# An attention kernel over embedding rows: another layout of the tiles, no loop, and one gather in 256 replaced by row fetches

## The chip, the core and the metric

The kernel runs on one core of one Trainium2 chip. A core has engines that run their own instruction streams in order and meet through semaphores: TensorE (PE, matrix products), VectorE (DVE, elementwise work, 32x32 transposes, statistics), ScalarE (ACT, activations and copies), GpSimd (POOL, here the engine that issues indirect DMAs) and SyncE (SP, here the engine that issues plain DMAs). SBUF is the on-chip memory of 128 partitions, PSUM the accumulator memory that TensorE writes. The metric is the device time of one execution in microseconds (us); before the change the median of three runs is 32846.29 us.

## What is computed

A user's history of 200 items is weighted by a small network ("attention unit") against a candidate item, and the weighted sum goes through a three-layer head. The batch is 16384, the history length L is 200, an embedding row has D = 64 floats, and the item table has 100000 rows. `dice` is an activation with a mean and a variance over the batch.

```python
def dice(x, alpha, axis):
    mean = jnp.mean(x, axis=axis, keepdims=True)
    var = jnp.var(x, axis=axis, keepdims=True)
    p = jax.nn.sigmoid((x - mean) * jax.lax.rsqrt(var + EPS))
    return x * (p + alpha * (1.0 - p))
u, it, c = u_emb[user], i_emb[item], c_emb[cate]
h = i_emb[hist]                                     # (200, 16384, 64)
itb = jnp.broadcast_to(it[None], h.shape)
feat = jnp.concatenate([h, itb, h - itb, h * itb], axis=-1)
a = dice(feat @ au_W1 + au_b1, au_alpha, axis=1)    # 36 hidden units, moments over the batch
w = a @ au_W2 + au_b2
cur = jnp.sum(w * h, axis=0)
z = jnp.concatenate([u, it, c, cur], axis=-1)
z = dice(z @ W1 + b1, alpha1, axis=0)
z = dice(z @ W2 + b2, alpha2, axis=0)
return z @ W3 + b3
```

## The kernel before

**Tiling.** The batch is cut into ND = 8 chunks of 2048 rows; a chunk is a tile of 128 partitions by TD = 16 rows. One *step* k handles one chunk c of one history position l (k = 8 l + c), so there are 1600 steps. `ts(c, TD)` names the columns of a chunk.

**Prologue.** `table_rows` and `table_store` go through the item table in 49 blocks and write a DRAM tensor `table` whose row is the embedding (64 floats) and its product with the part of the first attention layer that depends on the history item alone (64 floats: 36 units and padding). At the same time POOL gathers the candidate item, user and category rows (3 x 8 x 16 gathers, `fetch_one`), and `keep_one` transposes them and stores them to DRAM (`xi`, `ucT`) or keeps them (`itT`). All transposes of this part (`transpose`, `transpose_back`, L223 and L231) work on 64 partitions, four instructions for a tile.

**A step.** `fetch(k)` issues 16 indirect DMAs on POOL (`gather`, L202), each of which brings 128 rows of `table` (512 B each) into `land[k % 12]`, and one plain DMA on SP (L369) that brings the item's part of the layer, `xi[c]`, into `xit[k % 2]`. Once the rows have landed, `turn` (L377, four transposes of 64 partitions by 1024 elements) brings them into the layout with features on partitions, `product` multiplies by the item and runs the matrix product into PSUM tile `px`, on top of `xit`, which ACT has copied there (L458). `hidden` adds the two parts of the hidden layer and takes batch statistics (L390, L392). When the eight chunks of a position are done, `moments` makes scale and shift from the statistics. Eight to ten steps later `weigh(k-10)` (L398 to L415 on DVE, after two activations on ACT, L448 and L451) applies dice, sums over the hidden units, and adds weight times row to `cur`. The gather of step k writes the buffer that tile k-12 has used; the last reader of that is `weigh(k-12)`, which runs in step k-2.

**Order.** All instructions are in a hand-written order (`manual_schedule`). The first 168 history positions run in a hardware loop, `For_i` at L498, of 24 positions an iteration (7 iterations); the last 32 are written out. `fetch_ids` (L213, SP) loads the indices of the next position once in eight steps; it waits until the gathers of the position before have read the index buffer.

**Head.** During the written-out steps the parts of the first head layer that don't depend on `cur` are computed (`base_of_layer1`, scratch tile `zt`). After the last gather the pipeline drains in ten steps that also do layer 1 (`layer1`, `keep1`), then layer 2 runs chunk by chunk (dice on ACT and DVE, four pairs of matrix products, L595 and L525 to keep the result and its statistics), then layer 3 (L604) and the store.

Of the kernel before, what the change touches and what calls it, by code (L numbers as in the profile page):

```python
# [20 lines left out]
LPB = 24  # L21
LAND = 12
EARLY = 4
# [5 lines left out]
def din_kernel(  # L29
# [50 lines left out]

    parts = [(0, S), (S, A - S)]

# [3 lines left out]
    blk_h = once.tile([P, P], F32, name="blk_h")  # L86
    blk_i = once.tile([P, P], F32, name="blk_i")
    blk_m = const.tile([P, P], F32, name="blk_m")
    au_w = once.tile([P, 4, A], F32, name="au_w")
    au_bias = const.tile([P, 1], F32, name="au_bias")  # L90
    au_al = const.tile([P, 1], F32, name="au_al")
    au_1al = const.tile([P, 1], F32, name="au_1al")
    au_w2 = const.tile([P, 1], F32, name="au_w2")
# [4 lines left out]
    for e in range(2):  # L98
        rows = au_W1.rearrange("(g d) a -> d g a", d=D)[e * S : (e + 1) * S]
        for g in range(2):  # L100
            r = quarter(e, g)
            nc.sync.dma_start(au_w[r], rows)
            for q, (a0, n) in enumerate(parts):
                c, a = quarter(q, g, n), slice(a0, a0 + n)
                nc.vector.tensor_add(blk_h[r, c], au_w[r, 0, a], au_w[r, 2, a])
                nc.vector.tensor_sub(blk_i[r, c], au_w[r, 1, a], au_w[r, 2, a])
                nc.vector.tensor_copy(blk_m[r, c], au_w[r, 3, a])
    for g in range(2):
        for q, (a0, n) in enumerate(parts):
            r, a = quarter(q, g, n), slice(a0, a0 + n)  # L110
            nc.sync.dma_start(au_bias[r], col(au_b1)[a])
            nc.sync.dma_start(au_al[r], col(au_alpha)[a])
            nc.sync.dma_start(au_w2[r], au_W2[a])
# [11 lines left out]
    idx = [const.tile([P, NT], I32, name=f"idx{i}") for i in range(IDX)]  # L125
    stats = [const.tile([P, 2 * ND, nc.vector.BN_STATS_DIM], F32, name=f"st{i}") for i in range(2)]
    rstds = [const.tile([P, 1], F32, name=f"rs{i}") for i in range(2)]
    shifts = [const.tile([P, 1], F32, name=f"sh{i}") for i in range(2)]
    px, pz = (psum.tile([P, CD], F32, name=n) for n in ("px", "pz"))
# [6 lines left out]
    ucT = dram.tile([2, ND, P, CD], F32, name="ucT")  # L136
# [72 lines left out]
    def load_ids(t, ids):  # L209
        nc.sync.dma_start(t, ids.rearrange("(p n) -> p n", n=NT))  # L210

# [3 lines left out]
    def by_tile(t, i):  # L215

        return t[:, ts(i, CH)].rearrange("p (n t) -> p n t", t=S)

    def transpose(dst, rows, n=TD):

        for i in range(2):
            for e in range(2):
                nc.vector.transpose(  # L223
                    by_tile(dst[ts(e, D)], i)[:, :n], rows[ts(i, D), :n, ts(e, S)]
                )

    def transpose_back(rows, src, n=TD):

        for i in range(2):
            for e in range(2):  # L230
                nc.vector.transpose(  # L231
                    rows[ts(i, D), :n, ts(e, S)], by_tile(src[ts(e, D)], i)[:, :n]
                )

    def layer(dst, pairs, n=CH, onto=False):

        for i in range(2):
            cols = slice(i * CH, i * CH + n)
# [19 lines left out]
    ids = [once.tile([P, NT], I32, name=f"ids{i}") for i in range(3)]  # L258
    for t, v in zip(ids, (r_item, r_user, r_cate)):
        load_ids(t, v)  # L260
# [11 lines left out]
    def table_rows(b):  # L272
# [11 lines left out]
        transpose(rT, tab, m)  # L284
        layer((px, pz)[b % 2], [(blk_h, rT)], n=m * S)
        tabs[b] = tab, m

    def table_store(b):
        n0, n = blocks[b]
        tab, m = tabs.pop(b)  # L290
        transpose_back(tab[:, :, D:], (px, pz)[b % 2], m)
# [9 lines left out]
    def keep_one(j):  # L301
        c, k = j % ND, j // ND
        if k == 0:
            transpose(itT[:, c], land[j % EARLY])
            layer(ph, [(blk_i, itT[:, c])])
            t = pre.tile([P, CD], F32, tag="t", name="t")
            nc.scalar.activation(t, ph, AF.Identity, bias=au_bias)
            nc.scalar.dma_start(xi[c], t)
        else:
            t = pre.tile([P, CD], F32, tag="t", name="t")  # L310
            transpose(t, land[j % EARLY])
            nc.scalar.dma_start(ucT[k - 1, c], t)
# [22 lines left out]
    with ExitStack() as main:  # L335
# [15 lines left out]
        layer(px, [(blk_m, hx[0][:, 0])])  # L351
        nc.vector.bn_stats(stats[-1 % 2][:, 0, :], hx[0][:, 0, :CH])
        for c in range(1, 2 * ND):
            nc.vector.tensor_copy(stats[-1 % 2][:, c, :], stats[-1 % 2][:, 0, :])
        for i in range(2):
            nc.vector.memset(rstds[i], 0.0)
            nc.vector.memset(shifts[i], 0.0)
        nc.sync.dma_start(xit[-1 % XI], xi[ND - 1])

# [3 lines left out]
        def x_of(k):  # L363
            return land[k % LAND][:, :, D:]

        def fetch(k):
            l, c = divmod(k, ND)
            gather(land[k % LAND], idx[l % IDX][:, ts(c, TD)], table)
            nc.sync.dma_start(xit[k % XI], xi[c])  # L369

        def turn(k):

            rows = land[k % LAND].rearrange("p n (s e c) -> p n s e c", s=2, e=2)
# [64 lines left out]
        def step(k, last=None):  # L438
# [5 lines left out]
            if has(k):  # L444
                fetch(k)
# [207 lines left out]
```

## Time and profile before

| | |
|---|---|
| runs | 32784.65, 32846.29, 32846.42 us |
| profiled execution | 32783.09 us, its span 32780.9 us |
| first gather of the program, first and last gather of `table` (start) | 9.8, 490.4, 32514.0 us |
| POOL | busy 24515.6 us, 75% of the span |
| DVE | busy 25567.4 us, 78% |
| ACT | busy 7755.2 us, 24% |
| PE | busy 6366.6 us, 19% |
| DMA | 81 GB/s over the span |

A page of the profile lists instructions by line, engine, operation, tile and shape, with the number of them, their busy time, the mean duration of one, and the idle time of the engine just ahead of them with what ended it. "issue" as the end of an idle stretch means that nothing the profile shows was waited for. A timeline lists start, duration, engine, line, operation and tiles in order of time, with the idle time in brackets. `SPq` is the queue of DMAs that SP issues.

### The profile page before, as it was taken

What the parts mean: (1) busy time and instruction counts of PE and PEld (TensorE: products, weight loads), DVE (VectorE), ACT (ScalarE), POOL (GpSimd) and SP (SyncE); (2) the same over time, 40 slices, a digit from 0 to 9 for tenths busy, and PEclk for the clock granted to TensorE, in tenths of its full rate; (3) what the DMA queues carried; (4) which work ended last, traced back from release to release, by engine and by line L of the source; (5) the groups of instructions that cost most, each with busy time, mean ns of one, the idle gap of its engine ahead of it and who ended that gap; (6) DMA issues with size and microseconds to landing.
All of it is one profiled execution on the core that took longest, in us unless ns stands there. A gap on an engine that the chain in (4) does not pass through costs nothing. (4 is left out here: it accounts for less than half of the span.)

```text
span 32780.9 us, 100656 instructions
## 1 busy us (share of the span) xinstructions
PE 6366.6 (19%) x7006; PEld 2038.0 (6%) x7006; DVE 25567.4 (78%) x28797; ACT 7755.2 (24%) x7105; POOL 24515.6 (75%) x25991
## 2 busy tenths in 40 slices
PE   3111111111111111111111111111111112221112
PEld 0000000000000000000000000000000000000000
DVE  7777777777777777777777777777777777777777
ACT  1222222222222222222222222222222222222222
POOL 7777777777777777777777777777777777777775
PEclk5555555555555555555555555555555555555555
DMA  5222222222222222222222222222222223332222
GB/s 157 80 79 79 79 79 79 79 79 79 79 80 80 79 78 79 79 79 80 79 79 79 79 79 78 79 79 80 78 79 79 79 79 85 88 90 81 79 79 60
DMA packets 1214773, 2667.86 MB, mean 81 GB/s; under 512 B 551244, under 2 KB 577388, under 8 KB 1207916
## 3 DMA queue, kind: packets, MB, share of 16 engines
q0 software_dynamic: 831488, 1691.97, 19.6%
q1 hardware_dynamic: 372012, 906.09, 9.1%
q10 hardware_dynamic: 10560, 63.79, 0.5%
q14 instruction: 692, 5.67, 0.1%
q8 instruction: 21, 0.34, 0.0%
HBM read 2590.90 MB, written 69.16 MB: 81 GB/s over the span
## 5 line engine op out<-in xcount | busy, mean ns | idle before, releaser
L202 POOL DMA_INDIRECT land<-table,idx x25600 | 24152.2, 943 | 7872.6 <-issue 7703.8
L377 DVE STREAM_TRANSPOSE hx<-land 64x1024 f32<-64x1024 f32 x6404 | 7938.2, 1240 | 6360.3 <-DMA land<-table,idx 6218.5
L240 PE MATMUL px<-hx,blk_m 128*128 128x512 f32 x6408 | 5927.6, 1080 | 26007.0 <-DVE hx L384 25941.1
L448 ACT ACTIVATE pg<-land,sh,rs 128x1024 f32<-128x1024 f32 x1610 | 1943.8, 1207 | 12980.0 <-DVE cur L415 11593.3
L454 ACT COPY ph<-hx 128x1024 f32<-128x1024 f32 x1601 | 1627.6, 1017 | 10365.2 <-DVE hx L377 10362.2
L240 PEld LDWEIGHTS px<-hx,blk_m 128*128 128x128 f32 x6408 | 1880.1, 324 | 30022.8 <-issue 29846.4
L392 DVE BATCH_NORM_STATS2 st<-land 128x6 f32<-128x512 f32 x3204 | 2060.9, 685 | 55.0
L400 DVE STREAM_TRANSPOSE hx<-pg 128x1024 f32<-128x1024 f32 x1610 | 2011.7, 1250 | 55.2
L414 DVE TENSOR_TENSOR pg<-land,ph 128x1024 f32<-128x1024 f32 x1610 | 1977.8, 1228 | 55.0
L415 DVE TENSOR_TENSOR cur<-pg,cur 128x1024 f32<-128x1024 f32 x1610 | 1970.5, 1224 | 55.6
L402 DVE TENSOR_REDUCE r<-hx 128x32 f32<-128x1024 f32 x1610 | 1964.0, 1220 | 55.3
L390 DVE TENSOR_TENSOR land<-px,hx 128x1024 f32<-128x1024 f32 x1602 | 1961.6, 1224 | 49.5
L398 DVE TENSOR_TENSOR pg<-pg,land 128x1024 f32<-128x1024 f32 x1610 | 1968.8, 1223 | 2.7 <-ACT pg L451 2.5
L384 DVE TENSOR_TENSOR hx<-ph,itT 128x1024 f32<-128x1024 f32 x1601 | 1932.0, 1207 | 0.0
L451 ACT ACTIVATE pg<-pg,au_al,au_1al 128x1024 f32<-128x1024 f32 x1610 | 1895.0, 1177 | 54.3
L458 ACT COPY px<-xit 128x1024 f32<-128x1024 f32 x1601 | 1627.2, 1016 | 383.3 <-DVE land L390 381.1
L409 DVE SCALAR_TENSOR_TENSOR ph<-r,au_bias,r 64x16 f32<-64x16 f32 x3220 | 771.3, 240 | 114.8
L406 DVE COPY r<-r 64x32 f32<-64x32 f32 x1610 | 337.2, 209 | 55.0
L448 ACT ACT_TABLE_LOAD x209 | 268.1, 1283 | 452.6 <-DVE w1a L177 314.6
L249 ACT ACT_TABLE_LOAD x203 | 260.4, 1283 | 6.7 <-PE ph L555 3.2
L249 ACT ACTIVATE std<-var,eps 128x1 f32<-128x1 f32 x201 | 59.2, 295 | 475.2 <-DVE var L435 475.2
L425 DVE COPY other<-mv 32x2 f32<-32x2 f32 x804 | 155.6, 194 | 15.1
(122 smaller groups left out, 1885.8 us busy)
## 6 DMA issues: line engine op xcount, KB each, us to landing
xit<-xi SPq DMA_DIRECT2D x1601, 512.0 KB
land<-table,idx POOLq DMA_INDIRECT x25600
table<-tab ACTq DMA_DIRECT2D x48, 1024.0 KB
tab<-in_L_rec_i_emb SPq DMA_DIRECT2D x48, 512.0 KB
zt<-ucT SPq DMA_DIRECT2D x32, 512.0 KB
idx<-in_r_hist SPq DMA_DIRECT2D x200, 64.0 KB
ucT<-t ACTq DMA_DIRECT2D x16, 512.0 KB
zbase<-zt SPq DMA_DIRECT2D x10, 512.0 KB
```

The costliest lines, as they stand in the source:

```text
L202: nc.gpsimd.indirect_dma_start(out=dst[:, n, :], out_offset=None, in_=rows, in_offset=bass.IndirectOffsetOnAxis(ap=ids[:, n : n + 1], axis=0),
L240: nc.tensor.matmul(dst[:, cols], lhsT, rhs[:, cols], start=(j == 0 and not onto), stop=(j == len(pairs) - 1), skip_group_check=onto,)
L377: nc.vector.transpose(dst.rearrange("p s (n t) -> p n s t", t=S), rows[ts(i, D), :, :, e])
L384: nc.vector.tensor_mul(hm, ph, itT[:, k % ND])
L390: nc.vector.tensor_add(x_of(k), by_row(px), by_row(hx[k % 2][:, 1]))
L392: nc.vector.bn_stats(stats[l % 2][:, 2 * c + i, :], x_of(k)[:, ts(i, TD // 2)])
L398: nc.vector.tensor_mul(by_row(pg), by_row(pg), x_of(k))
L400: nc.vector.transpose(yT, pg)
L402: nc.vector.tensor_reduce(r, yT.rearrange("p (i n u) -> p i n u", i=2, u=S), mybir.AxisListType.X, ALU.add)
L414: nc.vector.tensor_mul(by_row(pg), rows, w.unsqueeze(2).to_broadcast([P, TD, D]))
L415: nc.vector.tensor_add(cur[:, ts(c, TD)], by_row(pg), cur[:, ts(c, TD)])
L448: nc.scalar.activation(by_row(pg), x_of(k - 10), AF.Sigmoid, bias=shifts[i], scale=rstds[i])
```

## The change

Four things change together.

1. **Layout.** A row's 64 features are split in two halves `e`, and the hidden units in two parts `q`; both lie along the free axis in place of the partitions ("four groups": the four groups of 32 partitions hold four groups of batch rows). So a transpose takes all 128 partitions in one instruction in place of two or four on 64 (`halves`, `of_rows`), the matrix product of a tile is four products accumulated over `e` (`first_layer`), weights, biases and statistics get a second column for `q`, and ACT's two activations of a step become four of half the width (`gates`). The sum over hidden units needs no copy across partitions any more. `moments` gathers the four groups with small copies. `turn` writes its first transpose to PSUM (`ph`), so that ACT's copy of it goes. Two PSUM tiles `pxs` alternate by step, except in the last 144 steps.
2. **No loop.** All 1600 steps are written out.
3. **Row fetches.** In every 16th step (k % 16 == 11, up to step 1440) the 16th gather is left out. Its 128 rows are fetched by SP with 128 DMAs of one row of 512 B, eight in each of the 16 steps before: a register load of eight addresses and eight DMAs with these registers, into one of two side buffers. These, and the addresses, lie in `zt`, which is free until the head. The addresses are loaded as indices six steps ahead (`load_addresses`, SP) and multiplied by 512 (`to_addresses`, DVE). ACT copies the side buffer to the place of the missing gather.
4. **Prologue and head.** The index loads are SP's first DMAs. Layer 2 of the head keeps a chunk's result two chunks later (`keep2`), and `dice` gives half of its tensor_scalar work to ACT.

The order within a step changes: `turn` and `product`, then `gates`, then SP's row fetches and the DMA of `xit`, then `weigh`, then `hidden`, and last ACT's copy of `xit` to PSUM.

```diff
+SIDES = ((16, 11),)
+ROW = 4 * 2 * D
+    def load_addresses(q, m):
+        l, c = divmod(m * SIDES[q][0] + SIDES[q][1], ND)
+        n = c * TD + TD - 1
+        ids = r_hist[ds(l, 1), :].rearrange("l (p n) -> l n p", n=NT)[:, n : n + 1]
+            nc.sync.dma_start(addr[q][m % 2].unsqueeze(1), ids)
+    def to_addresses(q, m):
+        nc.vector.tensor_scalar_mul(addr[q][m % 2], addr[q][m % 2], ROW)
+    def side_of(k):
+        for q, (every, at) in enumerate(SIDES):
+            if k % every == at and k < L * ND - SPAN - max(SIDES)[0]:
+                return q, k // every
+        return None
...
+        def rows_by_address(q, m, part):
+            dst = side[q][m % 2].bitcast(U8)
+            n = P // SIDES[q][0]
+            engine, kind = queues[q]
+            _, at = nc.values_load_multi_w_load_instructions(
+                addr[q][m % 2][:, ts(part, n)],
+                engines=(kind,), min_val=0, max_val=ROW * (V - 1),
...
+            for j, a in enumerate(at):
+                p = part * n + j
+                engine.dma_start(dst[p : p + 1], flat[ds(a, ROW)].rearrange("(o d) -> o d", o=1))
...
         def fetch(k):
             l, c = divmod(k, ND)
-            gather(land[k % LAND], idx[l % IDX][:, ts(c, TD)], table)
-            nc.sync.dma_start(xit[k % XI], xi[c])
+            n = TD - (side_of(k) is not None)
+            gather(land[k % LAND][:, :n], idx[l % IDX][:, c * TD : c * TD + n], table)
         def turn(k):
-            rows = land[k % LAND].rearrange("p n (s e c) -> p n s e c", s=2, e=2)
-            for i in range(2):
-                for e in range(2):
-                    dst = hx[k % 2][ts(e, D), :, ts(i, CH)]
-                    nc.vector.transpose(
-                        dst.rearrange("p s (n t) -> p n s t", t=S), rows[ts(i, D), :, :, e]
-                    )
-        def product(k):
-            hm = hx[k % 2][:, 0]
+            rows = land[k % LAND]
+            hm, hw = hx[k % 2][:, 0], hx[k % 2][:, 1]
+            nc.vector.transpose(halves(ph), of_rows(rows[:, :, :D]))
             nc.vector.tensor_mul(hm, ph, itT[:, k % ND])
-            layer(px, [(blk_m, hm)], onto=True)
+            nc.vector.transpose(halves(hw), of_rows(rows[:, :, D:]))
...
         def weigh(k):
-            nc.vector.tensor_mul(by_row(pg), by_row(pg), x_of(k))
-            yT = hx[k % 2][:, 0]
-            nc.vector.transpose(yT, pg)
+            nc.vector.tensor_mul(halves(pg), halves(pg), x_of(k))
+            nc.vector.transpose(x_of(k), halves(pg))
+            r = ph[:, :TD]
             nc.vector.tensor_reduce(
-                r, yT.rearrange("p (i n u) -> p i n u", i=2, u=S), mybir.AxisListType.X, ALU.add
+                r, land[k % LAND][:, :, D:], mybir.AxisListType.X, ALU.add
             )
-            r1 = small.tile([D, 2, TD], F32, tag="r1", name="r1")
-            nc.vector.tensor_copy(r1, r[D:])
-            w = ph[:, :TD]
-            for i in range(2):
-                nc.vector.scalar_tensor_tensor(
-                    w[ts(i, D)], r[:D, i], au_bias2[:D], r1[:, i], ALU.add, ALU.add
-                )
...
-            nc.vector.tensor_mul(by_row(pg), rows, w.unsqueeze(2).to_broadcast([P, TD, D]))
+            nc.vector.scalar_tensor_tensor(
+                by_row(pg), r.unsqueeze(2).to_broadcast([P, TD, D]), au_bias2, rows,
+                ALU.add, ALU.mult,
+            )
             nc.vector.tensor_add(cur[:, ts(c, TD)], by_row(pg), cur[:, ts(c, TD)])
...
             if has(k):
                 fetch(k)
             if has(k - 1):
                 turn(k - 1)
+                if not single(k - 1):
+                    product(k - 1)
+            if has(k - 10):
+                if k % ND == 2:
+                    moments((k - 10) // ND)
+                gates(k - 10)
+            if has(k):
+                if side_of(k):
+                    q, m = side_of(k)
+                    nc.scalar.copy(land[k % LAND][:, TD - 1], side[q][m % 2])
+                for q, (every, at) in enumerate(SIDES):
+                    m, part = divmod(k + every - at, every)
+                    if side_of(m * every + at):
+                        rows_by_address(q, m, part)
+                nc.sync.dma_start(xit[k % XI], xi[k % ND])
             if has(k - 10):
                 weigh(k - 10)
+            if has(k - 2):
+                hidden(k - 2, px_of(k - 2))
+            if has(k - 1) and single(k - 1):
+                preload(k - 1)
+                product(k - 1)
+            if has(k) and not single(k):
+                preload(k)
...
-        rest_l = L % LPB + LPB
-        with tc.For_i(0, L - rest_l, LPB) as l0:
-            with tc.manual_schedule():
-                for k in range(LPB * ND):
-                    fetch_ids(k, l0, LPB + 1)
-                    step(k)
...
-        K = rest_l * ND
+        K = L * ND
...
+            for c in range(ND + 2):
+                if c < ND:
+                    activated(c)
+                if c >= 2:
+                    keep2(c - 2)
```

## The prediction

> **What bounds the kernel now.** I read three views: the groups of instructions, the timeline of one step in the middle, and the list of waits.
>
> ```profile
> L202 POOL DMA_INDIRECT land<-table,idx x25600 | 24152.2, 943 | 7872.6 <-issue 7703.8
> L377 DVE STREAM_TRANSPOSE hx<-land 64x1024 f32<-64x1024 f32 x6404 | 7938.2, 1240 | 6360.3 <-DMA land<-table,idx 6218.5
> ```
>
> The first line is the gather. Busy and idle time together are 32024.7 us, nearly the span, and what ends its idle time is "issue", so no other engine holds it. 32024.7 / 25600 = 1.251 us a gather. DVE is busy for a larger share (78%), but its idle time ends with the landing of a gather: it waits for POOL.
>
> ```profile
> 20001.18 0.94 POOL L202 DMA_INDIRECT land<-table,idx  x1 [0.30 <-issue]
> 20001.31 5.00 DVE L377 STREAM_TRANSPOSE hx<-land 64x1024 f32<-64x1024 f32 x4 [4.21 <-DMA land<-table,idx]
> 20002.43 0.94 POOL L202 DMA_INDIRECT land<-table,idx  x1 [0.30 <-issue]
> 20003.67 0.94 POOL L202 DMA_INDIRECT land<-table,idx  x1 [0.30 <-issue]
> ...
> 20015.75 1.22 DVE L415 TENSOR_TENSOR cur<-pg,cur 128x1024 f32<-128x1024 f32 x1
> ```
>
> POOL goes on every 1.25 us without a break; 16 gathers make a step of 20.0 us (DVE's next step starts at 20021.30). DVE's step ends at 20016.97, so DVE has 4.3 us to spare in each. The starts of the gathers, read through the whole timeline, keep a mean distance of 1.2482 us, and of 1.2486 in the prologue, where DVE does other work.
>
> Only a few places break this rhythm: the loop's ends, here the second of seven, and the third tile (k = 2).
>
> ```profile
> 8174.25 0.94 POOL L202 DMA_INDIRECT land<-table,idx  x1 [0.30 <-issue]
> 8184.81 1.28 ACT L448 ACT_TABLE_LOAD   x1 [20.51 <-PEq L498]
> 8184.86 5.00 DVE L377 STREAM_TRANSPOSE hx<-land 64x1024 f32<-64x1024 f32 x4 [12.21 <-PEq L498]
> 8185.88 0.94 POOL L202 DMA_INDIRECT land<-table,idx  x1 [10.69 <-issue]
> ...
> 529.13 0.94 POOL L202 DMA_INDIRECT land<-table,idx  x1 [0.30 <-issue]
> 539.53 0.94 POOL L202 DMA_INDIRECT land<-table,idx  x1 [9.45 <-issue]
> ```
>
> 8174.25 to 8185.88 is 11.63 us in place of 1.25: 10.38 lost. Five loop ends are like this, the first lost 7.1 (8.36 between starts) and the last 3.1 (4.30): 62.1 us together. At k = 2 9.15 us are lost.
>
> So the span is: first gather at 9.8, 25984 gathers at 1.248, pauses, and 266.8 us after the start of the last gather (32514.03 to 32780.9).
>
> [...] the 25600 gathers take 938, 944 and 961 ns (minimum, median, maximum) whatever DVE runs. The change's large DVE instructions read one operand from PSUM, or have one input, or are adds with `pg` in PSUM, as before. [...] the trace has 1223 (L398), so I price DVE instructions of that size by the trace's rows. [...]
>
> **The change, part by part.**
>
> *Gathers removed.* k = 11, 27, ... 1435 are 90 steps, each with one gather less: 90 x 1.2482 = 112.3 us off the bound. The instructions in program order show 25510 gathers of `table`, and the first gather of a step waits for the scalar_tensor_tensor of `weigh(k-12)` as intended, two steps back.
>
> *Loop removed.* 62.1 us off the bound. The cost could come back as stalls of POOL's instruction fetch; against it stands that the 32 positions written out in the kernel before keep 1.2482 us as well. I take all 62.1; bound 0 to 62.1.
>
> *Layout.* DVE's step before, from the timeline: 5.00 + 1.23 + 1.29 + 1.21 + 1.22 + 1.25 + 1.22 + 0.18 + 0.52 + 1.23 + 1.22 = 15.6 us. After: `turn` 1.25 + 1.21 + 1.25, `weigh` 1.22 + 1.25 + 1.22 + 1.23 + 1.22, `hidden` 1.22 + 1.29: 12.4 us. The 3.2 us saved, 5.1 ms in all, buy nothing while POOL needs 20 us a step: DVE only waits longer. If gathers became cheap, 12.4 us would be next. ACT's copy to `ph` (1.02) goes; the four half activations cost about 0.75 each (between 295 ns at one element and 1207 at 1024, L249 and L448), 3.0 in place of 2.4. `moments` now stands ahead of `gates` in one step of eight, and DVE waits there for a table load, the square root, another table load and the gates, about 8 us: 20.4 us in that step, over 20.0 by less than the 7.6 that the other steps spare, and POOL asks for that buffer only two steps later. Nothing on the path.
>
> *Row fetches on SP.* Per step one load of eight registers, eight DMAs and `xit`. A DMA costs SP 0.32 to 0.43 us (L369, L102); [...] Each DMA waits for the DMA eight before it on SP, so `xit` waits for the first row's landing, some 2 us. Both ends: 4 us if the load is cheap, 11 us at 1 us a DMA and 3 us a load. SP has the time:
>
> ```profile
> SPq L369 <- ACT px L458: 24555.0, 1391, 22.0
> SPq L213 <- DMA land<-table,idx: 6095.4, 764, 28.6
> ```
>
> It spends 15 us of a step waiting for ACT, and once in eight steps up to 28.6 us for the index buffer. Behind that wait stand the next eight rows and `xit`, which ACT needs only at the end of the step, 12 us after the same landing. ACT's copy of the side buffer could wait for late rows and hold `turn`; the last rows are asked for a step before. Cost nothing. 11520 rows of 512 B are 5.9 MB beside 2668; the 16 engines are busy 29% of the time.
>
> *Prologue.* The indices go out first on SP: the first gather comes 1.96 us after that issue as before (7.87 to 9.83), so at 0.75 + 2.0 = 2.8: 7.0 us earlier. POOL bounds the prologue too (384 gathers x 1.2486 = 479.5), so faster transposes there are hidden, and the start of the main part moves by these 7.0.
>
> *The pause at k = 2.* That gather waits for `weigh(-10)` of step 0, which stands behind DVE's memsets. There are 16 bn_stats instead of one and 15 copies: 16 x 0.645 = 10.3 in place of 1.9, so +8.4. Step 0 up to the release: before 524.40 to 539.5 = 15.1, now 3.7 + 5.1 = 8.8, so -6.3. Pause 9.15 + 2.1 = 11.3.
>
> *Tail, draining.* From DVE's start at 32518.27 to the end of layer 1's statistics at 32643.6 it takes 125.3. After: step K 12.4; step K+1 ends at 23.9 because ACT's copy and gates come after `hidden`; `moments`, roots and gates to 31.0; `weigh` and transposes 9.1 to 40.1; seven steps of 6.2 + 2.86 + 1.27 = 10.35 make 72.5; the last layer-1 part 6.2. Sum 118.8: -6.5.
>
> *Tail, layer 2.* Before, every chunk waits in a ring: PE, then ACT's keep, then ACT's sigmoid, DVE, PE again.
>
> ```profile
> 32661.12 1.11 ACT L595 ACTIVATE land<-px,z2b 80x1024 f32<-80x1024 f32 x1 [8.98 <-PE px L240]
> 32662.13 1.23 ACT L563 ACTIVATE land<-land,zshift,zrstd 128x1024 f32<-128x1024 f32 x1
> ...
> 32665.57 1.99 PE L240 MATMUL pz<-land,w2a 128*80 128x512 f32 x2 [4.49 <-DVE land L565]
> ```
>
> One chunk takes 10.4 us from matmul to matmul, of which PE needs 5.9. With the keep two chunks later PE is the limit: 8 x 5.9 = 47.4 from 32655.15, plus 2.5 for the last keep and statistics, is 32705.1 in place of 32738.8: -33.7. Layer 3 stays bound by PE (27.5 us).
>
> *Sum*, against the profiled execution: 32783.1 - 112.3 - 62.1 - 7.0 + 2.1 - 6.5 - 33.7 = 32563.6 us, -0.67%. The runs: one lies at 32784.7, with the profiled one, and two are 61.7 higher, without a reason that the profile could show. That is close to the 62.1 of the loop's ends, and it may go with them, or remain. I stay with the low basis and let the range hold both.
>
> **The rivals.**
>
> *SP becomes the bound (slower).* Place: SP's queue between two `xit`. The path has 32563.6; 1440 steps have row fetches and average 19.89 us. SP takes over above 19.89 us a step, and from 20.05 the change is slower (220 us lost over 1440 steps). [...] For it: SP runs in order, `xit` stands behind eight DMAs of a kind that no trace shows. Against: three quarters of SP's time is free.
>
> *A slower gather.* Small descriptors on the 16 engines, or DVE's other access patterns, lengthen each gather. 8.5 ns (0.7%) eat the gain; at 10 ns, 32564 + 259 = 32820, no change. Against: the spread of 938 to 961 ns, and the same distance in the prologue at 69% DMA share as at 29% in the main part.
>
> *Half the gain.* The loop's 62.1 returns as fetch stalls or the 61.7 of the slower runs stays: 32626. For it: two of three runs.
>
> **How the numbers follow.** Forecast 0.77, half the gain 0.14, slower gather 0.04, SP as bound 0.05. Forecast's own range: gather distance +-0.5 ns is +-13, tail +-15, start +-10: 32530 to 32600. With the half case 32530 to 32650, which leaves less than 2 in 10 out. No change is within 0.2% (66 us) of 32846, about what a measurement of this kernel can tell: faster 0.92, same 0.03 (most of the slower gather), slower 0.05.
>
> **What would show it.** 25510 table gathers still 1.248 us apart and "issue" ahead of them; no pause every 24 positions; DVE idle 7 us a step for a landing; SP's wait for ACT still above 8 us a step; the last gather 226.6 us ahead of the end. Wrong, if POOL's gathers wait for DVE or ACT in the middle of the span, if SP has no idle time, or if the gather's duration moves by more than 5 ns.

## The result, and the profile after

| | before | after |
|---|---|---|
| runs | 32784.65, 32845.6, 32846.29, 32846.42 us | 32621.53 to 32623.08 us (4) |
| median | 32845.94 us | 32622.44 us |
| ratio | | 0.9934, interval 0.992 to 0.9949 |
| profiled execution, its span | 32783.09, 32780.9 us | 32622.16, 32620.4 us |
| gathers of `table` | 25600 | 25510 |
| mean distance of two gathers, pauses left out | 1.2482 us | 1.2506 us |
| start of the first gather of `table`; start of the last to the end | 490.4; 266.8 us | 489.6; 210.7 us |
| DVE, POOL, ACT, PE busy | 78, 75, 24, 19% | 63, 75, 22, 30% |

The change made the kernel 0.7% faster; the forecast was 32564 us, with a range of 32530 to 32650. In the first two of the three sessions of experiments below the kernel before took some 12% longer (36.8 and 36.9 ms; the chip of the second ran it in 32.8 ms in the third), and the others with it, so a time from these is set only against the kernel before in its own session.

The groups of instructions of the kernel after (busy time, mean ns, then the idle time ahead of them and what ended it):

```profile
L215 POOL DMA_INDIRECT land<-table,idx x25510 | 24125.4, 946 | 7795.9 <-issue 7575.2
L432 DVE STREAM_TRANSPOSE ph<-land 128x1024 f32<-128x1024 f32 x1601 | 2013.6, 1258 | 10395.8 <-DMA land<-table,idx 10199.7
```

The gathers still fill POOL: 24125.4 + 7795.9 = 31921 us, all the time from the first of them to the last, and "issue" ends most of the idle time. DVE now waits 10199.7 us for landings, 6.4 us for each of the 1601 `turn`s. What is new is the last digit of the mean: 946 ns in place of 943. It looks like nothing, but the mean distance has grown by 2.4 ns (the table above), and 25900 gathers make some 62 us of that.

SyncE, which now issues eight row fetches a step, in the list of waits (total us, number, longest) and in the list of one tile's instructions (minimum, median and maximum in ns):

```profile
SPq L542 <- ACT px L518: 16559.7, 1062, 45.9
SPq L223 <- DMA land<-table,idx: 8844.2, 483, 47.3
...
L415 SPq DMA_DIRECT2D zt<-table x11520: 222/228/343, 532.3 to 29063.7; - x199
L408 SPq TENSOR_LOAD <-zt x1440: 683/717/994, 531.5 to 29060.6; - x180
```

It still waits 10.3 us a step for ACT. The load of eight addresses takes 0.72 us and a fetch comes every 0.32 us or so, so the step's additions are some 3.3 us. SyncE's two largest waits together, 24555.0 + 6095.4 us before and 16559.7 + 8844.2 us after, have shrunk by as much: 5246.5 us, 3.3 us for each of the 1600 steps.

The start, in the timeline:

```profile
2.81 1.09 POOL L215 DMA_INDIRECT land<-in_L_rec_i_emb,ids  x1 [2.35 <-DMA ids<-in_r_item]
4.21 0.94 POOL L215 DMA_INDIRECT land<-in_L_rec_i_emb,ids  x1 [0.30 <-issue]
4.21 6.88 DVE L132 MEMSET cur<- 128x8192 f32 x1 [1.66 <-issue]
5.46 6.53 POOL L215 DMA_INDIRECT land<-in_L_rec_i_emb,ids  x1 [0.30 <-issue]
```

The first gather starts 7.0 us earlier than before (9.83), but the third lasts 6.53 us instead of 0.94, and so most of the early start is lost again: the first gather of `table` comes 0.9 us earlier. Further on, two gaps:

```profile
528.35 0.95 POOL L215 DMA_INDIRECT land<-table,idx  x1 [0.30 <-issue]
...
532.34 19.79 SPq L415 DMA_DIRECT2D zt<-table  x48
...
540.63 0.95 POOL L215 DMA_INDIRECT land<-table,idx  x1 [11.34 <-issue]
...
552.17 0.37 SPq L542 DMA_DIRECT2D xit<-xi  x1
...
556.08 1.02 ACT L518 COPY px<-xit 128x1024 f32<-128x1024 f32 x1 [25.54 <-DMA xit<-xi]
...
560.22 1.23 DVE L459 TENSOR_TENSOR pg<-pg,land 128x1024 f32<-128x1024 f32 x1 [13.00 <-ACT pg L452]
...
566.10 0.94 POOL L215 DMA_INDIRECT land<-table,idx  x1 [5.77 <-issue]
```

The first gap is the pause at k = 2, 12.28 - 1.25 = 11.03 us. The second, of 5.46 us at k = 3, was not there before. Read it upwards: POOL waits for the buffer that DVE's `weigh` frees, that waits for ACT's gates, ACT for `xit`, and `xit` stands on SP's queue behind a burst of 48 row fetches: 40 ahead of step 0, for the steps that the first side tile lacks, and step 0's own eight. Both gaps are marked "issue" although POOL waited for DVE, so the prediction's reading that "issue" means "no other engine holds it" is not safe by itself; in the middle, where every gap has the same 0.30 us, it holds. After 566.10 no two gathers start more than 1.92 us apart until the last; the pauses at the loop's ends are gone.

In the tail, layer 2's first chunks on PE, after:

```profile
32547.14 1.99 PE L275 MATMUL px<-land,w2a 128*80 128x512 f32 x2 [7.00 <-DVE land L665]
32548.93 1.91 PE L275 MATMUL px<-land,w2b 128*80 128x512 f32 x2
32550.63 1.82 PE L275 MATMUL px<-land,w2a 128*80 128x512 f32 x2
32552.29 1.02 PE L275 MATMUL px<-land,w2b 128*80 128x512 f32 x2
32553.15 1.02 PE L275 MATMUL px<-land,w2a 128*80 128x512 f32 x2
...
32576.60 1.02 PE L275 MATMUL ph<-land,w2b 128*80 128x512 f32 x2
```

After three pairs (1.99 to 1.82 us) the matmuls take about half as long, 1.02 us a pair, and stay so for the rest of the layer, in which PE no longer pauses between chunks. Before, PE paused for 4.5 to 6.6 us between two chunks, and seven of the eight began with a pair of 1.96 to 1.99 us. The prediction shows the first pair of the second chunk (1.99 us after a pause of 4.49); these are its others:

```profile
32667.36 1.91 PE L240 MATMUL pz<-land,w2b 128*80 128x512 f32 x2
32669.06 1.49 PE L240 MATMUL pz<-land,w2a 128*80 128x512 f32 x2
32670.39 1.02 PE L240 MATMUL pz<-land,w2b 128*80 128x512 f32 x2
```

One line of each kernel, before and then after, cut to layer 2 by windows (start and end, length, busy us and number for PE, weight loads, DVE, ACT, POOL, then PE's granted clock):

```profile
32653.00:32739.00 86.00, 47.33 (x64) 13.87 (x64) 28.03 (x36) 17.92 (x16) 0.00 (x0) 0.68 0.00 0
```

```profile
32547.00:32580.00 33.00, 30.40 (x64) 10.08 (x64) 21.70 (x28) 22.12 (x20) 0.00 (x0) 0.92 0.00 0
```

The same 64 matmuls are 47.33 us of PE at a mean clock of 0.68 and 30.40 at 0.92.

### The profile page after: what moved, and what is told of

Read it like the earlier page. It is cut to its first block, busy times and chain, and to the rows that moved or that the text cites. A ratio compares the mean times of both kernels' runs of the same rounds, so it can differ in the third digit from the quotient of the medians.

```text
span 32620.4 us, 131677 instructions
## 1 busy us (share of the span) xinstructions
PE 9909.9 (30%) x13650; PEld 3850.9 (12%) x13650; DVE 20471.7 (63%) x21563; ACT 7147.2 (22%) x8824; POOL 24495.3 (75%) x25901
## 4 chain that ended last, share of the span: by engine, by line
POOL 58%; issue 22%; DVE 13%; DMA 6%; ACT 0%; PE 0%; SPq 0%; POOLq 0%; DVEq 0%; ACTq 0%
POOL land L215 58%; DMA land<-table,idx 6%; DVE pg L467 1%; DVE land L460 1%; DVE ph L462 1%; DVE ph L432 1%; DVE cur L471 1%; DVE hx L433 1%; DVE pg L459 1%; DVE hx L434 1%; DVE land L439 1%; DVE st L441 1%; ACT pg L447 0%; ACT pg L452 0%; PE px L716 0%
## 5 line engine op out<-in xcount | busy, mean ns | idle before, releaser
L215 POOL DMA_INDIRECT land<-table,idx x25510 | 24125.4, 946 | 7795.9 <-issue 7575.2
L265 PE MATMUL px<-hx,blk_m 128*128 128x512 f32 x12824 | 9466.6, 906 | 22413.9 <-DVE hx L433 20403.5
L432 DVE STREAM_TRANSPOSE ph<-land 128x1024 f32<-128x1024 f32 x1601 | 2013.6, 1258 | 10395.8 <-DMA land<-table,idx 10199.7
L265 PEld LDWEIGHTS px<-hx,blk_m 128*128 128x128 f32 x12824 | 3674.9, 302 | 28203.0 <-issue 23274.9
L447 ACT ACTIVATE pg<-land,fac 128x512 f32<-128x512 f32 x3220 | 2508.6, 779 | 88.2 <-DVE cur L471 25.0
L459 DVE TENSOR_TENSOR pg<-pg,land 128x1024 f32<-128x1024 f32 x1610 | 1938.8, 1204 | 932.9 <-ACT pg L452 932.7
L452 ACT ACTIVATE pg<-pg,au_al,au_1al 128x512 f32<-128x512 f32 x3220 | 2419.2, 751 | 106.6
L467 DVE SCALAR_TENSOR_TENSOR pg<-ph,au_bias,land 128x1024 f32<-128x1024 f32 x1610 | 2081.8, 1293 | 57.2
L460 DVE STREAM_TRANSPOSE land<-pg 128x1024 f32<-128x1024 f32 x1610 | 2011.7, 1249 | 55.4
L462 DVE TENSOR_REDUCE ph<-land 128x16 f32<-128x1024 f32 x1610 | 1976.7, 1228 | 55.3
L434 DVE STREAM_TRANSPOSE hx<-land 128x1024 f32<-128x1024 f32 x1601 | 1975.4, 1234 | 0.0
L265 PE MATMUL px<-rT,blk_h 128*128 128x512 f32 (+1 forms) x392 | 221.1, 726 | 171.7 <-DVE rT L316 171.7
```

What stands on the lines that cost most here:

```text
L215: nc.gpsimd.indirect_dma_start(out=dst[:, n, :], out_offset=None, in_=rows, in_offset=bass.IndirectOffsetOnAxis(ap=ids[:, n : n + 1], axis=0),
L265: nc.tensor.matmul(dst[:, q * CH : q * CH + n], blk[:, e, q], rhs[:, e * CH : e * CH + n], start=(e == 0 and not onto), stop=(e == 1), ski ...
L432: nc.vector.transpose(halves(ph), of_rows(rows[:, :, :D]))
L434: nc.vector.transpose(halves(hw), of_rows(rows[:, :, D:]))
L447: nc.scalar.activation(halves(pg)[:, q], x_of(k)[:, q], AF.Sigmoid, bias=facs[i][:, 1, q : q + 1], scale=facs[i][:, 0, q : q + 1],)
L452: nc.scalar.activation(pg[:, ts(q, CH)], pg[:, ts(q, CH)], AF.Identity, bias=au_al[:, q : q + 1], scale=au_1al[:, q : q + 1],)
```

## The experiments

Open after the result were three things. The gathers are 2.4 ns further apart: is that the change's doing? The row fetches: do they really cost nothing? And the two new losses at the start: are they what the timeline suggests?

### First session: both kernels again, and one part of the change at a time

The kernel before and the kernel after, unchanged.

> The kernel before, unchanged, for a second profile. The runs of before lie on two levels, 32784.7 and 32846, and the profiled one is on the low one. The kernel after has gathers 1.2507 us apart instead of 1.2482; 2.5 ns x 25,900 = 63 us. Theory A (the distance belongs to the chip or the execution, not to the change): this run shows 1.2507 us and about 32846 us whenever the kernel after on the same chip shows 1.2507. Theory B (the change lengthens the gather): this run shows 1.2482 us and about 32784 us beside a kernel after of 1.2507.

> The kernel after, unchanged, on the same chip. Theory A: the same distance of gathers as the kernel before on this chip, and 221 to 224 us less time. Theory B: 1.2507 us whatever the kernel before shows, 32622 us.

The changed kernel without row fetches, all 1600 tiles gathered:

```diff
-SIDES = ((16, 11),)
+SIDES = ()
```

> The kernel after without row fetches: all 25600 gathers of the table on POOL. If the row fetches cost nothing but the start, 90 x 1.2507 = 112.6 us are lost and the 5.5 us pause at the fourth tile is won back: 32729 us. If the row DMAs lengthen each gather (a form of theory B), the distance falls to 1.2482 and the time is 63 us lower, 32666 us.

The kernel before without the loop; the head's base is worked on in the last 256 steps, as before:

```diff
-        rest_l = L % LPB + LPB
-        with tc.For_i(0, L - rest_l, LPB) as l0:
...
+        rest_l = L
...
-                next(work, None)
+                if k >= K - 256:
+                    next(work, None)
```

> The kernel before with all 1600 steps written out, nothing else. My prediction: 62.1 us less than the kernel before on the same chip (32784 if that one has 32846), no pause in the gathers after the start. If the loop's cost comes back as stalls of instruction fetch: less than 62, down to 0, with gathers further apart. If the two levels of the kernel before come from its loop's ends, and not from the distance of the gathers, this kernel has the distance of 1.2482 and 32722 us.

Measured, against a median of 36779.15 us for the kernel before in the first session (median, ratio and its interval): before again 36779.49 (1.000, interval 0.999 to 1.0009); after again 36929.81 (1.004, 1.0025 to 1.0056); without row fetches 36674.26 (0.9973, 0.9959 to 0.9986); before without the loop 36717.74 (0.9983, 0.9976 to 0.9991).

Without the loop the kernel before gets 61.4 us faster, against 62.1 read from the pauses of the first profile. The rest differs from what the result would have one expect: here the whole change is 151 us slower, and leaving the row fetches out gains 256. The undisturbed gathers, those that follow within 1.27 us, were 1.2482 us apart in both forms of the kernel before (as in the first profile) and 1.2508 us in the kernel after (1.2506 in the result). Without row fetches the distance did not fall (1.2517 us). That spoke for a property of the program other than the row fetches, and the next session was to find which.

### Second session: the place of the indices, and the row fetches again

The kernel after once more:

> The changed kernel once more, because on the chip of the first experiments it came out 0.4% slower than the kernel before and on the chip of the result 0.7% faster. Theory P (the gather distance itself is a property of the program): wherever this runs, the undisturbed distance of two gathers is 1.2506 us (duration 945.7 ns), as it was twice, against 1.2482 us for the kernel before. Theory Q (the sign of the change is a property of the chip): where the kernel before takes near 32.8 ms the ratio is 0.993; where it takes near 36.8 ms the ratio is 1.004. Rival to Q: the 1.004 was an accident of one execution, and the ratio is 0.993 wherever it runs.

The index tiles back behind the land tiles:

```diff
-    idx = [const.tile([P, NT], I32, name=f"idx{i}") for i in range(IDX)]
     ids = [once.tile([P, NT], I32, name=f"ids{i}") for i in range(3)]
...
     land = [const.tile([P, TD, 2 * D], F32, name=f"land{i}") for i in range(EARLY)]
+    idx = [const.tile([P, NT], I32, name=f"idx{i}") for i in range(IDX)]
```

> The changed kernel with the two index tiles idx put back to their place in SBUF behind the land tiles (as in the kernel before), nothing else moved. If the 2.3 ns that each gather has become longer come from the place of the indices: duration 943.4 ns, distance 1.2482 us, and 25300 x 2.4 ns = 62 us less than the changed kernel. Rival (they come from something else that both four-group kernels share, such as the place of the land tiles or the numbers of the landing semaphores): 945.7 ns, and the time of the changed kernel within 10 us.

The kernel without row fetches again:

> The changed kernel with no row fetches, all 1600 tiles gathered. Theory 'the row fetches cost nothing' (the prediction's): 90 gathers more, 90 x 1.2506 = 112 us slower than the changed kernel, less 5.5 us for the pause at k=3 that the burst of row fetches makes, so 107 us slower. Rival (the row fetches take time of the gathers, as the 255 us on the first chip suggest): less than 60 us slower, or faster.

Sixty-four row fetches a step in steps 4 to 399, none later (the addresses are loaded eight at a time, and the start is the edited one of the third session):

```diff
-SIDES = ((16, 11),)
+SIDES = ((2, 1),)
...
-            if k % every == at and k < L * ND - SPAN - max(SIDES)[0]:
+            if k % every == at and k >= 2 * every and k < 400:
...
-                for ahead, make in ((6, load_addresses), (4, to_addresses)):
+                for ahead, make in ((2, load_addresses), (1, to_addresses)):
```

> The changed kernel with one tile in every 2 steps fetched by SyncE in steps 4 to 399, 64 row fetches per step in place of 8 (none after step 400; the first burst is left out and the start's two moments edits are in). From the trace of the changed kernel a step then holds on SyncE 64 x 0.323 + 8 loads of 8 addresses x 0.8 + 0.36 = 27.4 us against 15.5 gathers x 1.2506 = 19.4 us. Theory 'SyncE becomes the bound where its step is longer than the gathers': the 396 steps run at 27 us each, and the kernel is about 396 x 8 = 3.1 ms slower than the changed kernel. Rival (row fetches overlap on the queue, so that the true issue cost is lower): under 20 us a step, and about 200 us faster.

Measured, against 36913.49 us for the kernel before in the second session: after 37028.73 (1.0031, 1.0018 to 1.0044); indices back 37041.11 (1.0033, 1.0023 to 1.0043); without row fetches 36707.55 (0.9943, 0.9927 to 0.996); 64 fetches a step 42546.82 (a single run).

The place of the indices is not it: 944.86 ns for the undisturbed gathers with them moved, 944.87 without. And theory P, that the distance belongs to the program, fell with the trace of the kernel after: it had a third distance here, 1.2496 us.

The row fetches cost 321 us here, against the prediction's "Cost nothing". In both sessions the whole change loses, and without its row fetches it gains, so here they are the part that loses. SyncE's queue in the timeline shows why this is not carried over to the result; first the kernel after in the profiled execution of the result, then in the second session:

```profile
10007.86 0.35 SPq L542 DMA_DIRECT2D xit<-xi  x1
10009.09 2.91 SPq L415 DMA_DIRECT2D zt<-table  x8
```

```profile
10003.63 20.32 SPq L415 DMA_DIRECT2D zt<-table  x8
10026.05 0.70 SPq L542 DMA_DIRECT2D xit<-xi  x1
```

The same eight fetches stretch over 20.32 us instead of 2.91; the median fetch keeps SyncE for 0.70 us in the second session and for 0.23 in the result. Why is not known. No cause is drawn from these two sessions for what row fetches cost; the question went to the third.

With 64 fetches, the line of windows shows the stretch of 6 ms in which they run:

```profile
2000.00:8000.00 6000.00, 971.93 (x1299) 375.04 (x1299) 2044.82 (x2205) 725.56 (x953) 2368.70 (x2511) 0.57 0.16 43
```

POOL has 2511 instructions there, 15.5 to a step, which makes 6000 x 15.5 / 2511 = 37.0 us a step: far above POOL's 19.4. SyncE's waits for others come to 111.5 us in all of these 6000; the largest:

```profile
SPq L417 <- DMA zt<-table: 100.3, 208, 1.4
```

SyncE does become the bound when its step is longer than the gathers, as the first rival had it. The 27.4 us expected were too few for the second session, and 64 fetches were not run without its stretching. An estimate from this trace's medians, 2.61 us for eight fetches and 0.94 us from these to the next eight, is 28.4 us a step, still above POOL's 19.4.

### Third session: the start, and 4, 8 and 16 row fetches a step

Three edits at the start:

```diff
-    nc.vector.memset(cur, 0.0)
...
+            if j == 2:
+                nc.vector.memset(cur, 0.0)
...
-        for q in range(2):
-            for c in range(ND):
-                nc.vector.bn_stats(stats[-1 % 2][:, q, c, :], hx[0][:, 0, :CH])
+        nc.vector.bn_stats(stats[-1 % 2][:, 0, 0, :], hx[0][:, 0, :CH])
+        for m in range(1, 2 * ND):
+            nc.vector.tensor_copy(stats[-1 % 2][:, m // ND, m % ND, :], stats[-1 % 2][:, 0, 0, :])
...
-            if k % every == at and k < L * ND - SPAN - max(SIDES)[0]:
+            if k % every == at and k >= every and k < L * ND - SPAN - max(SIDES)[0]:
...
-            for part in range(every - at):
-                rows_by_address(q, 0, part)
```

> The changed kernel with three edits at its start: the memset of cur is moved from beside the third gather to a later place in the prologue; of the 16 bn_stats that fill the first moments one is left and 15 small copies spread its result; the burst of 48 row fetches ahead of step 0 is left out, so the first such tile is gathered. From the trace of the changed kernel: third gather 6.53 to about 1.25 us (-5.3), pause before k=2 from 11.0 to about 4.5 us (-6.5), pause at k=3 of 5.46 us gone (-5.5), one gather more (+1.25): -16 us against the changed kernel. Rival (the pauses have another cause): the third gather stays at 6.5 us, or the pause at k=3 stays.

With these, a tile in every 32 steps, and a tile in every 8 steps (the addresses are then loaded four at a time, and eight at a time):

```diff
-SIDES = ((16, 11),)
+SIDES = ((32, 27),)
```

> As e3_start, but one tile in every 32 steps fetched by SyncE, 4 row fetches per step instead of 8: about half as many gathers saved. Where the kernel before takes near 36.8 ms, the trace shows one engine taking its instructions at multiples of 0.70 us: VectorE before, GpSimd without row fetches, SyncE with 8 row fetches per step. Theory L (there the engine with the longest list of instructions sets the pace, and 8 fetches make that SyncE): with 4 fetches SyncE has 11 instructions a step instead of 19, GpSimd is the longest again at 1.40 us per gather, and the time is that of the kernel without row fetches less 43 x 1.40 = 60 us, so below both kernels. Rival (every row fetch costs the gathers about the same, 320 us for 8 per step): without row fetches + 160 - 60 = 100 us more. Where the kernel before takes near 32.8 ms: 45 gathers x 1.25 = 56 us above e3_start in both theories.

```diff
-SIDES = ((16, 11),)
+SIDES = ((8, 7),)
```

> As e3_start, but one tile in every 8 steps fetched by SyncE, 16 row fetches per step. Where the kernel before takes near 32.8 ms: 16 x 0.323 + 2 loads x 0.8 + 0.36 = 7.1 us of SyncE in a step of 19.9, so hidden: 90 gathers less again, -112 us against e3_start. Rival there (the fetches slow the gathers): not faster than e3_start. Where it takes near 36.8 ms, theory L: SyncE has 36 instructions a step and the time rises by more than 300 us over e3_start. Rival there (the cost comes once, from having any fetches): within 100 us of e3_start.

The kernel after with one line moved:

```diff
             if has(k):
+                nc.sync.dma_start(xit[k % XI], xi[k % ND])
                 if side_of(k):
...
-                nc.sync.dma_start(xit[k % XI], xi[k % ND])
```

> The changed kernel with the fetch of xit issued on SyncE ahead of the step's row fetches instead of behind them; nothing else. Theory M (row fetches cost time where they do because xit, which the step's gates wait for, stands behind them on SyncE's queue): where the kernel before takes near 36.8 ms, at least half of the 320 us between the changed kernel and the one without row fetches goes. Theory L (SyncE has too many instructions a step, in whichever order): within 60 us of the changed kernel, ratio 1.003. Where the kernel before takes near 32.8 ms: only the pause at k=3 changes, under 6 us, in both theories.

Measured, against 32784.84 us for the kernel before in the third session (six of its seven runs lie between 32783.47 and 32786.05, one at 32816.78):

| kernel | median us | ratio, interval | gathers of `table` |
|---|---|---|---|
| `xit` first | 32554.54 | 0.993, 0.9913 to 0.9946 | 25510 |
| start edits, 8 fetches a step | 32543.09 | 0.9926, 0.991 to 0.9943 | 25511 |
| start edits, 4 fetches a step | 32599.12 | 0.9943, 0.9927 to 0.996 | 25557 |
| start edits, 16 fetches a step | 32429.94 | 0.9892, 0.9875 to 0.9908 | 25420 |

**Row fetches.** From 4 to 8 fetches a step 46 gathers go and 56.0 us; from 8 to 16 another 91 gathers and 113.2 us. That is 1.22 and 1.24 us for each gather replaced, nearly all of the 1.25 us that one takes. No kernel without row fetches ran in the third session; that the first four a step cost nothing either is read from the trace of the result, whose terms add up below. SyncE's wait for ACT, with 16 fetches a step:

```profile
SPq L544 <- ACT px L520: 11382.2, 1036, 45.6
```

It has shrunk from 16559.7 to 11382.2 us, and 7.1 us a step are left. With 16 a step the kernel beats both others. Theories L and M, which were about times near 36.8 ms, were not put to the test here, and stay open.

**The start.** In the kernel with the start edits:

```profile
2.92 1.09 POOL L214 DMA_INDIRECT land<-in_L_rec_i_emb,ids  x1 [2.46 <-DMA ids<-in_r_item]
5.05 0.95 POOL L214 DMA_INDIRECT land<-in_L_rec_i_emb,ids  x1 [0.16 <-issue]
6.31 0.94 POOL L214 DMA_INDIRECT land<-in_L_rec_i_emb,ids  x1 [0.30 <-issue]
...
58.31 6.88 DVE L360 MEMSET cur<- 128x8192 f32 x1 [1.66 <-issue]
58.81 0.94 POOL L214 DMA_INDIRECT land<-in_L_rec_i_emb,ids  x1 [0.30 <-issue]
60.06 0.94 POOL L214 DMA_INDIRECT land<-in_L_rec_i_emb,ids  x1 [0.30 <-issue]
...
526.60 0.95 POOL L214 DMA_INDIRECT land<-table,idx  x1 [3.23 <-issue]
```

No gather lasts 6.5 us, the pause at k = 2 has fallen from 11.0 to 2.9 us (4.5 expected), and nothing holds POOL at k = 3. The kernel is 11.5 us faster than the one with `xit` first; the edits were to bring 16 over the kernel after, of which `xit` first shares 5.5. That kernel keeps the gather of 6.5 us and the pause at k = 2, and has lost the pause at k = 3, which shows the chain over SP's queue. Why the third gather took 6.5 us is not settled. Its end is tied to the memset beside it: in all seven traces with the start of the kernel after it ended 0.88 to 0.89 us after the memset, though it began anywhere from 5.46 to 5.59 us. Yet the second gather ran its 0.94 us beside the same memset, and so do those at 58 us.

**The distance of the gathers.** The groups of the kernel with `xit` first, then of the one with the start edits:

```profile
L215 POOL DMA_INDIRECT land<-table,idx x25510 | 24069.3, 944 | 7786.1 <-issue 7643.7 <-DMA land<-table,idx 72.8 <-DVE st L441 50.3
```

```profile
L214 POOL DMA_INDIRECT land<-table,idx x25511 | 24104.2, 945 | 7777.5 <-issue 7601.7 <-DMA land<-table,idx 96.9 <-DVE st L442 66.1
```

The first is the changed kernel but for one line moved on SP, and its gathers are 1.2483 us apart: the distance of the kernel before. So the change does not lengthen them, and the program does not fix the distance: the kernel after itself had 1.2506, 1.2508 and 1.2496 us in its three profiled executions, one on each occasion. The second, with `xit` in its old place, ran its profiled execution in 32577.76 us, 1.2496 us apart, and its three others in 32541.58 to 32543.22. The 35 us between are 1.36 ns for each of 25900 gathers, about the difference of the two distances, so by its times the distance went with the execution of one and the same kernel. The kernels with 4 and with 16 fetches did the same: their profiled executions, with 1.2495 and 1.2496 us, took 31 to 32 us more than most of the others. The kernel before has 32784.84 us in most runs of the third session, 32816.78 in one, and 32846 in three of the four runs beside the result: the same steps of 32 and 62 us, though only one of these executions was profiled. What sets the step was not found.

## Why the prediction was right

**The sum.** At equal distances the gain that was forecast is met: the medians beside the result, both on the upper step if the times are read so, differ by 223.5 us, and in the third session the kernel with `xit` first is 230.3 us below the kernel before, 224.8 without the 5.5 of its own edit. The forecast had 219.5. Item by item, from the two traces:

| term | forecast | measured |
|---|---|---|
| gathers removed | -112.3 | -112.3 (90 fewer; 1.24 us each between 8 and 16 fetches) |
| loop removed | -62.1 | -62.1 in the trace; -61.4 alone |
| first gather earlier | -7.0 | -0.9 at the first of `table` |
| pause at k = 2 | +2.1 | +1.9 |
| pause at k = 3 | none | +5.5 |
| tail, draining and layer 1 | -6.5 | -4.1 |
| tail, layer 2 | -33.7 | -50.3 |
| tail, rest | 0 | -1.7 |
| distance of the gathers | 0 | +63 |

The loop's row is shown by a run of its own, in the first session, and the row fetches' by the third session; the tail's rows are read from the two traces alone. The last row is why the time was 32622 and not 32564. The forecast stayed on "the low basis", that of the profiled execution of before, while the runs of the result show the higher distance. The prediction had this in its third rival, as "the 61.7 of the slower runs stays", and 32626 was that rival's time. The rival was named "half the gain", though, and this is not what happened: the 62 us lie on both kernels, and the gain is whole. The other half of that rival, fetch stalls of written-out code, is refuted by the loop's removal alone: 61.4 of the 62.1 us came. Why the loop's ends cost this no run shows; what the trace names there is PE's sequencer at the loop's own line (L498), at the second end for 12.21 us of DVE's idle time and 20.51 of ACT's.

Some of the agreement is luck. The forecast's own range, 32530 to 32600, missed the time; only the range widened for this rival holds it. Layer 2 gave 16.6 us more than forecast, the start and the rest of the tail 12.1 us less, and these errors nearly cancel. And three of the four runs of the kernel before lay on the upper step, like all of the kernel after: against the one run below, 32784.65, the same kernel gains 162 us. The sum was right in what it took off the bound, the gathers and the loop, 174.4 of its 219.5 us.

**Layer 2 was mis-sized.** The step "PE is the limit: 8 x 5.9" took 5.9 us a chunk from a stage in which PE stood still for 4.5 us or more before every chunk. Without these pauses all eight chunks took 30.5 us (32547.14 to 32577.62), not 47.4. In the trace of the kernel after PE's granted clock is 0.50 from 32547 to 32552 us, behind a pause of 7.0 us, and 1.00 from 32552 to 32577: the slow pairs (1.99 to 1.82 us) last 5.1 us here before those of 1.02. The price of an operation was taken together with the stall that the change removes.

**The first gather.** The step "7.0 us earlier" was right for the first gather, and was lost at the third. The prediction had priced what moves to the front at the even pace of the gathers, and left no term for what else this moves together; what held the third gather is open.

**The pause at k = 3.** It counted SP's load for a step in the middle, and said that `xit` is needed late. At the start there is no slack yet: the 48 fetches of the first tile, 19.79 us on SP, stand ahead of a step's `xit`.

**SyncE.** "Cost nothing" holds in the middle of the span, and for 16 fetches too, where the kernel before takes 32.8 ms; it does not hold at the start, nor in the first two sessions. The forecast's ends were 4 and 11 us a step, and about 3.7 were measured: the load of eight addresses takes 0.72 us, 90 ns an address, and a fetch comes every 0.32 us, the low end of the 0.32 to 0.43 that the prediction read from other DMAs. Nor does `xit` wait some 2 us a step for the first row: its waits for rows (`SPq L542 <- DMA zt<-table`) are 52, of 0.5 us at most and 10.2 us together.

**The rivals.** SyncE as the bound did not come about at 8 fetches (nor at 16), and did at 64. A slower gather was there by 2.4 ns, below the 5 ns that were to refute the prediction, and not because of the change. DVE's saved 3.2 us a step went into waiting, as forecast: 6.4 us a step for landings and 0.6 for ACT's gates (L459), where 7 for landings were forecast.

## What to carry to other kernels

When one engine issues without a break, count what is issued and what interrupts it, and price both on the same basis for both kernels: a difference of 2 ns in an operation that runs 26000 times is as large as one of the gains here, and by the runs here it went with the execution, not with the change. Compare runs at equal pace before any of it is put down to a change. A price read in a stage with stalls contains them (here PE's granted clock, 0.68 with the pauses and 0.92 without), so an operation that will run without pauses has to be priced where it already does. And a queue that is idle most of the time can still be late once, where its work comes in a burst before the pipeline is full (here 48 fetches, 19.79 us). Last, work that is hidden on one engine stays hidden only while that engine keeps its pace: where SyncE's fetches were stretched, the same change lost 0.3 to 0.4%.

## What the runs showed of the hardware

- The distance of identical indirect gathers on POOL came in steps, 1.2482, 1.2496 and 1.2506 us, and one kernel can be on different ones in different executions: the kernel after had 1.2506 us in the result and 1.2496 in the second session.
- A DMA issued by SyncE with a register address takes 0.228 us (median) and comes every 0.32 us (rows of 512 B). With sixteen a step the gathers were 1.2496 us apart, with four and eight 1.2495 and 1.2496 in the same session.
- Eight addresses are loaded into SyncE's registers in 0.72 us.
- A gather of 6.39 to 6.53 us, seven times the usual length, stood third in every profiled kernel that starts as the kernel after does, always ended 0.88 to 0.89 us after a memset of 6.88 us beside it, and went when the work around it was moved; the gather before it ran beside the same memset in its usual time.
- PE's pairs of matmuls took 1.99 us after a pause of 7.0 us and 1.02 us from 5.1 us on; with pauses of 4.5 us or more between chunks, 64 matmuls took 47.33 us of PE, without them 30.40.
- In two sessions the eight fetches of a step stretched (20.32 us in place of 2.91 in the lines shown). The chip of the second of them ran everything at the usual times in the third.
